# Startup loads of a window-attention and Fourier kernel: the table of positions moves to ScalarE's DMA queue, three weights move to SyncE's, and VectorE scales the odd heads' keys in three more rows

## The chip, the cores and the metric

The kernel runs on one core of one Trainium2 chip, as one program. The metric is the device time of one execution in microseconds (us). Before the change four runs took 3613.70, 3613.27, 3615.47 and 3615.18 us, a median of 3614.44.

A core has five engines that each follow their own stream of instructions in order: TensorE (PE) multiplies matrices and transposes, with its weight loads (PEld) beside the multiplications; VectorE (DVE) and ScalarE (ACT) do element-wise work; GpSimd (POOL) does element-wise work on data outside PSUM; SyncE (SP) does little but issue DMA transfers. In this kernel transfers are issued by SyncE and, at the start alone, by ScalarE; each of the two has a queue of its own (q1 and q10 in the profile). An engine that issues a transfer spends time of its own stream on it.

## The reference, cut to what matters

The input is 32 images of 56 x 56 positions with 128 channels, all in float32. Two layers follow one another, and each adds its result to its input:

```python
x = x + _L0_conv_ref(_gn(x), rpb_table, w_qkv, w_proj, b_proj)   # window attention
x = x + _L1_conv_ref(_gn(x), w0, w1, W1, b1, W2, b2)             # Fourier mixing, feed-forward
```

`_gn` is a group norm over 32 groups of 4 channels of one image. The first layer rolls the image by 3 in both directions, cuts it into 8 x 8 windows of 49 positions, and attends inside each window with 4 heads of 32 channels:

```python
attn = einsum('bhid,bhjd->bhij', q * scale, k) + bias[None] + mask
out  = einsum('bhij,bhjd->bihd', softmax(attn), v)
```

`bias` is gathered from the table of relative positions, `rpb_table` (169 x 4), one value for each pair of positions in a window and each head. `mask` is -100 between positions that the roll brought together. The second layer takes a cosine transform along each of the two axes, keeps 32 modes, multiplies each by a 128 x 128 matrix, transforms back, and applies a feed-forward net with 512 hidden channels.

## The kernel before, in words

**Tiling and stages.** An image has 8 rows of 8 windows, and a cycle of the main loop (line 1020) takes one row further. Image 0 goes through the attention alone, in `first_rows` (line 967, cycles 0 to 10). From cycle 11 on each cycle works on a row of attention of one image and on parts of the Fourier layer and feed-forward of the images before it, in `halves_first`, `eighths`, `quarters`, `full` and `halves_last`. Ahead of cycle 0 `image_groups` transposes image 0 in four groups of two rows (TensorE, line 276), ScalarE copies the result out (lines 288 to 294), VectorE gathers statistics (line 298), and `image_norm` (line 316) turns these into a factor for each channel, which ScalarE multiplies into the weights of queries, keys and values (`wn`, line 364).

**One row of attention.** `attn_qk` (line 372) multiplies the row by the weights of the queries and of the keys (helper at line 112) and copies both out of PSUM. The queries go out in one ScalarE pass (line 380). The keys go out twice, once with the odd heads set to zero and once with the even heads set to zero, by a factor of 0 or 1 per channel (`heads`) and a bias (`im.bias`): `k_sb[:, 0]` on ScalarE (line 389), and `k_sb[:, 1]` on ScalarE (line 393) where `first` is true, on VectorE (line 397) where it isn't. `first_rows` passes True and `halves_first` False. `attn_scores` (line 418) multiplies queries and keys, and VectorE adds the table `bm` to the result (line 439). Then follow the maximum (VectorE, line 449), its subtraction (POOL, line 450), the exponential (ScalarE, line 456), the sum and its reciprocal (VectorE, lines 461 and 463), and the multiplication (POOL, line 464). One cycle later the result is transposed (line 475), then multiplied by the values (line 500) and projected.

**The table `bm`.** `bm` holds bias plus mask for each kind of row and window. It is made at the start, in four steps. Seven small DMAs read the shifted table of positions into seven partitions (`rpb_cols`, line 166): those with an even index are issued on SyncE's queue, the odd ones on ScalarE's. Seven more spread this over 49 partitions (`rpb`, line 170), and one copies those to a second set of 49 (line 173). All of these eight are on SyncE's queue, and so are the four reads of the mask (line 181). VectorE then makes sixteen additions of bias and mask (line 191): eight on the first set of partitions and eight on the second. A second part of `bm`, for the last row of windows, is added by POOL in cycles 4 and 5.

**Other loads.** `load_image(0)` (line 126) issues five DMAs on SyncE's queue: half of image 0 (784 KB), most of the other half (672 KB), and three small pieces around the roll's edge. `const_load` (line 132) loads the constants: those named in `FIRST`, that is `gavg` (64 KB), `wqkv` (192 KB) and `bproj` (56 KB), on ScalarE's queue, all others on SyncE's. On SyncE's queue the tables of the cosine transforms, image 1 and the weights of the second layer follow.

**What sets the order.** The main loop stands inside `manual_schedule` for TensorE, ScalarE, VectorE and POOL: these keep the order in which it is written. What comes before the loop (the constants, `bm`) and everything on SyncE is placed by the framework's planner, which works with its own costs when the program is built. So SyncE's order, and the place of the sixteen additions in VectorE's stream, aren't written in the code. Waits between engines are made by the framework. The semaphores of the DMAs are handed out in turn, eight of them, over both queues together.

Of the kernel before, what the change touches and what calls it, by code (L numbers as in the profile page):

```python
# [48 lines left out]
def swin_fourier_kernel(  # L49
# [20 lines left out]
    nc = tc.nc  # L70
# [12 lines left out]
    def attn_bank():  # L83
        return bank("pa", 4)
# [23 lines left out]
    def halved(dst, lhsT, rhs, start=True, stop=True):  # L108

        for p in range(0, dst.shape[0], P // 2):  # L110
            ps = slice(p, min(p + P // 2, dst.shape[0]))
            nc.tensor.matmul(dst[ps], lhsT=lhsT[:, ps], rhs=rhs, start=start, stop=stop)  # L112
# [14 lines left out]

    FIRST = ("gavg", "wqkv", "bproj")  # L130

    def const_load(shape, src, name):
        t = const.tile(shape, F32, tag=name, name=name)
        (nc.scalar if name in FIRST else nc.sync).dma_start(t, src)
        return t

    ident = const.tile([P, P], F32, tag="ident", name="ident")
# [7 lines left out]
    gavg = const_load([P, P], group_avg, "gavg")  # L145
    wqkv = const_load([P, 3 * C], w_qkv_t, "wqkv")
    wproj = const_load([P, C], w_proj_t, "wproj")
    bproj = const_load([TC, C], b_proj.partition_broadcast(TC), "bproj")

# [7 lines left out]
    with nc.allow_non_contiguous_dma(reason="relative position bias, once"):  # L157


        cols = work.tile([P, 4, C], F32, tag="zT", name="rpb_cols").rearrange("p n c -> p (n c)")  # L160
        cols = cols[:WS, : NH * span * WS].rearrange("p (h y x) -> p h y x", h=NH, y=span)
        for ix in range(WS):
            src = bass.AP(
                rpb_rev.tensor, rpb_rev.offset + WS - 1 - ix, [[span, NH * span], [1, WS]]
            )
            (nc.scalar if ix % 2 else nc.sync).dma_start(
                cols[ix : ix + 1].rearrange("p h y x -> p (h y) x"), src.unsqueeze(0)
            )
        for iy in range(WS):
            nc.sync.dma_start(  # L170
                rpb[iy * WS : (iy + 1) * WS], cols[:, :, WS - 1 - iy : span - iy]
            )
# [37 lines left out]
    with nc.allow_non_contiguous_dma(reason="constant, once"):  # L210
        for blk in range(8):
# [4 lines left out]
            src = idct_h.rearrange("p (h r) -> p h r", r=4)[modes, :, 2 * li : 2 * li + 2]  # L216
# [85 lines left out]
    def image_bias(im, i):  # L302

        n0, n1 = WS * i // 2, WS * (i + 2) // 2
        for a, e in ((n0, n0 + 4), (n0 + 4, n1)):
            piece = im.x[:, a:e]
            nc.gpsimd.tensor_tensor(  # L307
                piece, piece, bproj.unsqueeze(1).to_broadcast([TC, e - a, C]), ALU.add
            )
# [62 lines left out]
    def attn_qk(im, i, first):  # L372

        n = RT if i else RT + 1
        q, src = q_sb, im.xw[i][:, :n]
        pq = attn_bank()
        halved(pq[:, :n], im.w[:, 0:C], src)
        if i == 0:
            nc.scalar.mul(im.bias[:, 0:1], pq[:, RT:n], QS)
        nc.scalar.activation(  # L380
            q[:, :RT], pq[:, :RT], AF.Identity, bias=im.bias[:, 0:1], scale=QS
        )
        pk = attn_bank()
        halved(pk[:, :n], im.w[:, C : 2 * C], src)
        if i == 0:
            for u in range(2):
                nc.scalar.mul(im.bias[:, 3 + u : 4 + u], pk[:, RT:n], heads[:, u : u + 1])
        pk3 = pk[:, :RT].rearrange("p (w j) -> p w j", j=WT)
        nc.scalar.activation(
            k_sb[:, 0], pk3, AF.Identity, bias=im.bias[:, 3:4], scale=heads[:, 0:1]  # L390
        )
        if first:
            nc.scalar.activation(
                k_sb[:, 1], pk3, AF.Identity, bias=im.bias[:, 4:5], scale=heads[:, 1:2]
            )
        else:
            nc.vector.tensor_scalar(
                k_sb[:, 1], pk3, heads[:, 1:2], im.bias[:, 4:5], ALU.mult, ALU.add
            )
# [18 lines left out]
    def attn_scores(im, i, r):  # L418

        q, a = q_sb, a_sb[r % 3]  # L420

        ps = [attn_bank(), attn_bank()]
        for pr in range(NP):
            for hp in range(2):
                cs = HALVES[hp]
                for e in range(2):
                    w = 2 * pr + e  # L430
                    nc.tensor.matmul(  # L431
                        ps[hp][HALVES[e], pr * 2 * WT : (pr + 1) * 2 * WT],
                        lhsT=q[cs, w * WT : w * WT + JP],
                        rhs=k_sb[cs, :, w],
                        start=True,
                        stop=True,
                    )
        for hp in range(2):
            nc.vector.tensor_tensor(  # L439
                a[:, 2 * hp : 2 * hp + 2, :, 0:WT].rearrange("p u w j -> p w u j"),  # L440
                ps[hp][:, :RT].rearrange("p (w u j) -> p w u j", u=2, j=WT),
                bm[:, i // (NWR - 1), hp],
                ALU.add,
            )

    def attn_max(r):
        a3 = a_sb[r % 3].rearrange("p t w j -> p (t w) j")[:, :, 0:WT]
        mx = small.tile([P, 2 * NWR], F32, tag="mx", name="mx")
        nc.vector.tensor_reduce(mx, a3, axis=AX.X, op=ALU.max)  # L449
        nc.gpsimd.tensor_tensor(  # L450
            a3, a3, mx.unsqueeze(2).to_broadcast([P, 2 * NWR, WT]), ALU.subtract
        )

    def attn_exp(r):
        a3 = a_sb[r % 3].rearrange("p t w j -> p (t w) j")[:, :, 0:WT]
        nc.scalar.activation(a3, a3, AF.Exp)  # L456

    def attn_divide(r):
        a3 = a_sb[r % 3].rearrange("p t w j -> p (t w) j")[:, :, 0:WT]
        sm = small.tile([P, 2 * NWR], F32, tag="sm", name="sm")  # L460
        nc.vector.tensor_reduce(sm, a3, axis=AX.X, op=ALU.add)  # L461
        rs = small.tile([P, 2 * NWR], F32, tag="rs", name="rs")
        nc.vector.reciprocal(rs, sm)  # L463
        nc.gpsimd.tensor_tensor(  # L464
            a3, a3, rs.unsqueeze(2).to_broadcast([P, 2 * NWR, WT]), ALU.mult
        )

    def attn_transpose(im, i, r):

        a = a_sb[r % 3]  # L470
        im.aT[i] = []
        for hf in range(2):
            pt = attn_bank()
            for h in range(NH):
                nc.tensor.transpose(  # L475
                    pt[:PW, h * P : h * P + PW],
                    a[:PW, h, 2 * hf : 2 * hf + 2].rearrange("p w j -> p (w j)")[:, :PW],
                    ident[:PW, :PW],
                )
            aT = work.tile([P, 4, P], F32, tag="aT", name="aT", bufs=4)  # L480
            src = pt[:PW].rearrange("p (m x) -> p m x", x=P)[:, :, :PW]
            if hf:
                nc.scalar.copy(aT[:PW, :, :PW], src)  # L483
            else:
                nc.vector.tensor_copy(aT[:PW, :, :PW], src)
            im.aT[i].append(aT)
# [335 lines left out]
    def row(r):  # L822
        return (images[r // NWR], r % NWR) if 0 <= r < NB * NWR else (None, 0)
# [143 lines left out]
    def first_rows(cycle, norm):  # L967
        im, i = row(cycle)
        if im:
            attn_qk(im, i, True)  # L970
        if cycle:
            attn_exp(cycle - 1)
        im3, i3 = row(cycle - 3)
        if im3:
            attn_values(im3, i3, cycle - 3)
        im2, i2 = row(cycle - 2)
        if im2:
            attn_transpose(im2, i2, cycle - 2)
        if cycle:
            attn_divide(cycle - 1)  # L980
        if im:
            attn_scores(im, i, cycle)
            attn_max(cycle)
        if im3:
            attn_project(im3, i3)
        next(norm, None)
        last, j = row(cycle - 4)
        if last:
            for _ in attn_sums(last, j):
                pass  # L990
        if im:
            attn_v(im, i, cycle)

        if cycle < NWR // 2:
            image_bias(im, 2 * cycle)
        elif cycle >= NWR - 2 and cycle < NWR + 2:
            image_bias(images[1], 2 * (cycle - NWR + 2))
        if cycle in (4, 5):
            for half in range(2):
                bias_and_mask(nc.gpsimd, 1, cycle - 4, half)  # L1000
        next_begin(cycle)
        next_groups(cycle)
        if cycle == CONV_BEGIN - 1:
            start_stats(im3)
            for _ in attn_sums(im3, i3):
                pass
            attn_exp(cycle)
            attn_divide(cycle)
            last, j = row(cycle - 1)
            attn_transpose(last, j, cycle - 1)  # L1010

    ET = mybir.EngineType
    with tc.manual_schedule(engines={ET.PE, ET.Activation, ET.DVE, ET.Pool}):
# [6 lines left out]
        for cycle in range(NB * NWR + CONV_BEGIN + FF_AT[-1] - NWR + 1):  # L1020
# [22 lines left out]
            b, i = divmod(cycle, NWR)  # L1043
# [65 lines left out]
```

## Time and profile before

| | |
|---|---|
| median of four runs | 3614.44 us |
| the profiled execution | 3613.70 us |
| its span, first to last instruction | 3611.8 us |
| TensorE busy | 3551.5 us (98%) |
| VectorE busy | 2251.4 us (62%) |
| ScalarE busy | 2144.3 us (59%) |
| POOL busy | 1374.1 us (38%) |
| DMA, mean rate over the span | 108 GB/s |

The profile is one execution, seen by the hardware's profiler. Times count from the first instruction. A busy share is a mean over the whole span. The chain of work is followed back from the last instruction: at each step to what released it, or to the instruction before it on the same engine. In a timeline row the first number is the start, the second the length. "x7" means seven instructions put together, and what stands in brackets is the engine's idle time before them with what ended it. SPq and ACTq are issues of DMAs by SyncE and ScalarE. In a list of waits the numbers are the sum, the count and the longest.

The first instructions of the start, as the timeline tells them: the image's DMAs are issued from 0.74 us on. TensorE begins its transposes at 7.09 us, when the first half has landed, and goes on with the second half at 10.62. VectorE's norm runs from 14.60 to 17.16, ScalarE writes the scaled weights at 17.90, the keys and queries are multiplied from 18.57, and the first scores from 23.11. The bias is first added at 26.29. The rows of image 0 then follow one another: the first maximum of image 0 (line 449) begins at 27.37, that of image 1 at 84.5. From image 3 on an image takes 110.1 to 112.8 us.

### The profile page before, as it was taken

The numbers are of one execution on the slowest core, as the hardware profiler recorded it, in microseconds if no ns is written. First come the engines' busy times: TensorE is split into PE (matmuls) and PEld (weight loads), VectorE is DVE, ScalarE is ACT, GpSimd is POOL, SyncE is SP. The second block draws the span as 40 slices with busy tenths as digits, with TensorE's granted clock in tenths as the row PEclk, the third lists the DMA queues.
The fourth block names the chain that finished last, engine by engine and source line by source line (L and its number), as shares of the span: only waits on it lengthen the run. The fifth ranks groups of instructions, "written<-read, shape, count | busy, mean of one in ns | idle before, by whom it ended". The sixth has DMA issues, their size and how long they took to land.

```text
span 3611.8 us, 161664 instructions
## 1 busy us (share of the span) xinstructions
PE 3551.5 (98%) x72192; PEld 2829.2 (78%) x72192; DVE 2251.4 (62%) x4722; ACT 2144.3 (59%) x4044; POOL 1374.1 (38%) x1437
## 2 busy tenths in 40 slices
PE   7899999999999999999999999999999999999999
PEld 5777778787878787887777787878877877777776
DVE  7766666666666666666656666666666666666641
ACT  5566565655666655666656665556665566655553
POOL 5443343433444333434334434343443344342421
PEclk9999999999999999999999999999999999999999
DMA  4334443444434444334444344443444443444343
GB/s 118 95 103 111 112 112 94 114 112 111 112 97 110 110 112 115 102 104 109 112 108 113 98 110 112 111 117 93 112 109 115 106 115 94 113 109 114 94 116 98
DMA packets 687349, 390.30 MB, mean 108 GB/s; under 512 B 39967, under 2 KB 657600, under 8 KB 686400
## 3 DMA queue, kind: packets, MB, share of 16 engines
q1 hardware_dynamic: 686045, 379.65, 38.9%
q8 instruction: 568, 9.31, 1.1%
q14 instruction: 125, 1.02, 0.1%
q10 hardware_dynamic: 611, 0.32, 0.0%
HBM read 218.29 MB, written 161.48 MB: 105 GB/s over the span
## 4 chain that ended last, share of the span: by engine, by line
PE 93%; DVE 4%; issue 1%; ACT 1%; POOL 1%; DMA 0%; SPq 0%; POOLq 0%; DVEq 0%; ACTq 0%
PE pc L112 38%; PE pa L112 15%; PE pa L409 6%; PE pc L680 6%; PE pa L475 6%; PE pc L646 6%; PE pa L431 5%; PE pa L500 4%; PE pc L719 4%; PE pa L276 1%; PE pc L276 1%; DVE a L439 1%; DVE xf L730 0%; DVE oT L531 0%; POOL rstd L617 0%
## 5 line engine op out<-in xcount | busy, mean ns | idle before, releaser
L450 POOL TENSOR_TENSOR a<-a,mx 128x784 f32<-128x784 f32 x256 | 389.3, 1521 | 1392.4 <-DVE mx L449 959.8
L112 PE MATMUL pc<-wff,hid 128*64 128x128 f32 x12544 | 740.3, 273 | 1.3 <-ACT hid L764 1.0
L112 PE MATMUL pc<-xf,wff 128*64 128x512 f32 (+2 forms) x3584 | 718.5, 540 | 1.1 <-DVE xf L730 1.0
L112 PEld LDWEIGHTS pc<-wff,hid 128*64 128x64 f32 x12544 | 702.7, 137 | 7.7 <-ACT hid L764 4.6
L461 DVE TENSOR_REDUCE sm<-a 128x16 f32<-128x784 f32 x256 | 248.2, 970 | 675.9 <-ACT a L456 672.4
L464 POOL TENSOR_TENSOR a<-a,rs 128x784 f32<-128x784 f32 x256 | 389.2, 1520 | 606.6 <-DVE rs L463 555.0
L764 ACT ACTIVATE hid<-pc,b1sb 128x512 f32<-128x512 f32 (+2 forms) x896 | 522.3, 631 | 72.4 <-PE pc L112 68.9
L112 PEld LDWEIGHTS pc<-xf,wff 128*64 128x64 f32 x3584 | 278.0, 137 | 356.6 <-issue 236.8
L380 ACT ACTIVATE q<-pa,bqkv 128x392 f32<-128x392 f32 x256 | 150.3, 587 | 463.8 <-PE pa L112 458.0
L112 PE MATMUL pa<-xw,wn 128*64 128x392 f32 (+1 forms) x2048 | 389.2, 495 | 9.3 <-ACT wn L364 8.3
L531 DVE TENSOR_SCALAR oT<-pa,bqkv 128x98 f32<-128x98 f32 (+2 forms) x768 | 171.3, 278 | 242.7 <-PE pa L500 242.6
L456 ACT ACTIVATE a<-a 128x784 f32<-128x784 f32 x256 | 222.7, 870 | 146.8 <-POOL a L450 144.8
L752 POOL TENSOR_TENSOR res<-res,b2sb 128x512 f32<-128x512 f32 (+2 forms) x256 | 264.2, 1037 | 113.8 <-DMA res<-scr 113.8
L416 ACT COPY v<-pa 128x512 f32<-128x512 f32 x256 | 151.0, 590 | 244.9 <-PE pa L409 244.8
L409 PE MATMUL pa<-wn,xw 128*64 128x128 f32 x4096 | 283.0, 280 | 5.4 <-issue 3.7
L307 POOL TENSOR_TENSOR xl<-xl,bproj 112x512 f32<-112x512 f32 (+1 forms) x256 | 287.1, 1144 | 0.0
L500 PEld LDWEIGHTS pa<-aT,v 49*32 49x32 f32 x16384 | 172.3, 105 | 145.2 <-issue 119.1
L439 DVE TENSOR_TENSOR a<-pa,bm 128x392 f32<-128x392 f32 x512 | 265.1, 561 | 25.9 <-PE pa L431 2.2
L483 ACT COPY aT<-pa 113x452 f32<-113x452 f32 x256 | 139.6, 545 | 209.8 <-PE pa L475 206.3
L409 PEld LDWEIGHTS pa<-wn,xw 128*64 128x64 f32 x4096 | 220.8, 137 | 38.0 <-issue 4.8
L449 DVE TENSOR_REDUCE mx<-a 128x16 f32<-128x784 f32 x256 | 246.6, 963 | 4.3
L788 DVE TENSOR_TENSOR res<-pc,res 128x512 f32<-128x512 f32 (+3 forms) x257 | 138.6, 550 | 174.9 <-PE pc L112 129.8
(97 smaller groups left out, 5748.8 us busy)
## 6 DMA issues: line engine op xcount, KB each, us to landing
zscr<-z SPq DMA_DIRECT2D x512, 112.0 KB
htok<-scr SPq DMA_DIRECT2D x256, 196.0 KB
zT<-zscr SPq DMA_DIRECT2D x192, 256.0 KB
res<-scr SPq DMA_DIRECT2D x160, 256.0 KB
out_dram<-res SPq DMA_DIRECT2D x160, 256.0 KB
scr<-xl SPq DMA_DIRECT2D x128, 224.0 KB
xl<-in_x_dram SPq DMA_DIRECT2D x32, 784.0 KB
xl<-in_x_dram SPq DMA_DIRECT2D x32, 672.0 KB
```

Of the source, the lines that this page charges most:

```text
L112: nc.tensor.matmul(dst[ps], lhsT=lhsT[:, ps], rhs=rhs, start=start, stop=stop)
L307: nc.gpsimd.tensor_tensor(piece, piece, bproj.unsqueeze(1).to_broadcast([TC, e - a, C]), ALU.add)
L409: nc.tensor.matmul(pv[hs, j * C : (j + 1) * C], lhsT=im.xw[i][:, w * WT : w * WT + JP], rhs=im.w[:, 2 * C : 3 * C], start=True, stop=True,)
L439: nc.vector.tensor_tensor(a[:, 2 * hp : 2 * hp + 2, :, 0:WT].rearrange("p u w j -> p w u j"), ps[hp][:, :RT].rearrange("p (w u j) -> p w u ...
L449: nc.vector.tensor_reduce(mx, a3, axis=AX.X, op=ALU.max)
L450: nc.gpsimd.tensor_tensor(a3, a3, mx.unsqueeze(2).to_broadcast([P, 2 * NWR, WT]), ALU.subtract)
L456: nc.scalar.activation(a3, a3, AF.Exp)
L461: nc.vector.tensor_reduce(sm, a3, axis=AX.X, op=ALU.add)
L464: nc.gpsimd.tensor_tensor(a3, a3, rs.unsqueeze(2).to_broadcast([P, 2 * NWR, WT]), ALU.mult)
L500: nc.tensor.matmul(po4[u][h * HD : (h + 1) * HD, 2 * f + e], lhsT=v[ks, 2 * f + e, h * HD : (h + 1) * HD], rhs=im.aT[i][f][ks, h, e * JP : ...
L752: nc.gpsimd.tensor_tensor(res[:m, c0:c1], res[:m, c0:c1], b2sb[:m].unsqueeze(1).to_broadcast([m, c1 - c0, C]), ALU.add,)
L764: nc.scalar.activation(hf[:, :n], ph[:, :n], AF.Relu, bias=b1sb[:, f : f + 1])
```

## The change

Three edits. `const_load` issues all its DMAs on SyncE's queue: `gavg`, `wqkv` and `bproj` now stand there behind the five DMAs of image 0, which come first in the code. All seven reads of the table of positions into `rpb_cols` are issued on ScalarE's queue, so they are the only DMAs that ScalarE issues. And `first_rows` passes `cycle > 2` for `first`: in cycles 0, 1 and 2 the keys of the odd heads are copied by VectorE (line 397) instead of ScalarE (line 393).

```diff
-    FIRST = ("gavg", "wqkv", "bproj")
-
     def const_load(shape, src, name):
         t = const.tile(shape, F32, tag=name, name=name)
-        (nc.scalar if name in FIRST else nc.sync).dma_start(t, src)
+        nc.sync.dma_start(t, src)
         return t
...
-            (nc.scalar if ix % 2 else nc.sync).dma_start(
+            nc.scalar.dma_start(
                 cols[ix : ix + 1].rearrange("p h y x -> p (h y) x"), src.unsqueeze(0)
             )
...
         if im:
-            attn_qk(im, i, True)
+            attn_qk(im, i, cycle > 2)
         if cycle:
             attn_exp(cycle - 1)
```

The line numbers in the text are those of the kernel before.

## The prediction

> **What bounds the kernel now.** I read the page's chain of work first, then the same chain over the first 30 us, where the edit lies, and then the records of the queues there.
>
> The page gives the chain that ended last over the whole span: TensorE carries it, and no DMA queue has a share worth a percent.
>
> ```profile
> PE 93%; DVE 4%; issue 1%; ACT 1%; POOL 1%; DMA 0%; SPq 0%; POOLq 0%; DVEq 0%; ACTq 0%
> ```
>
> Over the first 30 us the chain is another one (start, length, what):
>
> ```profile
> 1.19 9.38 DMA xl<-in_x_dram
> ...
> 14.95 0.88 SPq L170
> ...
> 22.36 2.40 DMA rpb<-rpb
> ...
> 24.79 0.84 DVE bm L191 x5
> ...
> 26.29 0.03 DVE a L439
> ```
>
> The first scores are added to the bias at 26.29, and what comes last there is the table of positions: seven gathers on SyncE's queue, one copy of the table, VectorE's sixteen additions. After 26.29 the rows of image 0 hang on one another and TensorE takes over. No view shows a later stage that waits for a load set in motion at the start, so what row 0 wins or loses goes through to the end at full size.
>
> The timeline of ScalarE, SyncE and TensorE over the same stretch shows the second path to 26.29 and who issues what:
>
> ```profile
> 2.36 2.89 ACTq L166 DMA_DIRECT2D rpb_cols<-in_rpb_rev_dram  x3
> 5.29 1.28 ACT L294 ACT_TABLE_LOAD   x1 [5.29 <-issue]
> 9.67 3.46 SPq L166 DMA_DIRECT2D rpb_cols<-in_rpb_rev_dram  x4
> 13.25 1.52 SPq L181 DMA_DIRECT2D mask<-in_shift_mask_dram  x4
> 14.95 5.76 SPq L170 DMA_DIRECT2D rpb<-rpb_cols  x7
> 22.38 0.68 ACT L393 ACTIVATE k<-pa,bqkv,heads 128x392 f32<-128x392 f32 x1
> 23.11 1.59 PE L431 MATMUL pa<-k,q 64*64 64x98 f32 x32 [1.65 <-ACT k L393]
> ```
>
> The scores of row 0 end at 24.70, so they stood ready 1.55 us before the bias did. That slack is the first number.
>
> **Image and weights (removed from ScalarE's queue).** The DMA view (packets, MB, share of the 16 engines) up to 7 us, and then up to 10.6 us, when the image's second half had landed (10.57):
>
> ```profile
> q1 hardware_dynamic: 1913, 0.97, 52.9%
> q10 hardware_dynamic: 291, 0.26, 19.2%
> ```
>
> ```profile
> q1 hardware_dynamic: 3346, 1.67, 65.6%
> q10 hardware_dynamic: 611, 0.32, 16.5%
> ```
>
> q1 is SyncE's queue, q10 is ScalarE's queue: gavg, wqkv and bproj, 0.32 MB, moved while the image was still on its way, at 245 GB/s (2 to 7 us) with the engines' share at 1.00. Behind the image on SyncE's queue they no longer do: 0.32 MB / 245 GB/s = 1.3 us, second half at 9.3. Bounds: 0 (if the tail at 8.1 to 10.6, only 196 GB/s, is a few slow engines) and 1.6 us (at that 196). I take 1.3, since the share stood at 0.95 or over to the end. The first half lands about 1 us sooner too, but that is worth little: ident_x is done at 6.27 and TensorE began at 7.09.
>
> The Trainium skill ("Trainium Kernel Development and Optimization", Key Constraints) says that DMAs of several issuing engines run on the same 16 DMA engines, so that spreading them saves only the sequencer's time. Read strictly it speaks against this step: the half would stay at 10.57, row 0 would begin its bias at 24.9, and the time would be 3613.0. It says nothing on order, and the q10 rows show weights moved ahead of the image.
>
> **Seven reads of the table on ScalarE's queue.** ScalarE issues DMAs ahead of its own work. Out go 0.42 + 0.66 + 0.45, and four reads come: 0.73 + 1.34 + 6 x 0.76 + gaps = 6.8, where it was 5.25 (line 166 on ScalarE took 1.34 us the first time, 0.76 the median). The table load (1.28) then ends at 8.1, exactly when the first copy began (8.11). Its four groups of copies take 1.0 us each, so two end at 10.1 and the third waits for the image: TensorE from 9.3, copy from 10.4 (11.66 before). So the image's 1.3 us survive; norm, wn (17.90), keys and scores come 1.3 earlier. The cover is thin: each further us on ScalarE's queue up to 1.3 eats into the gain one for one. What could add it is this line of SyncE's waits:
>
> ```profile
> SPq L118 <- DMA gavg<-in_group_avg_dram: 2.9, 1, 2.9
> ```
>
> The semaphores go round in eight, and an issue waits until the transfer eight issues before it has landed. The seventh read has a first or second issue as its forerunner (landed by 6), about when it would be issued anyway.
>
> **The table's path on SyncE.** Four reads leave (3.46), gavg, wqkv and bproj come (1.53 with gaps 1.65). The weights are not needed soon: wqkv at 17.90, bproj by POOL at 29.95, wproj at 43.87, gavg at 104. One of the four weights has the image's second half as its forerunner, so the last of them is issued about 10.4, and the reads, out by 6.8, have landed by then. Gathers: seven at 0.82, 10.5 to 16.3 (14.95 to 20.71 before). If the masks follow (1.52), the copy is issued at 17.9 and lands 2.40 later, 20.3 (24.76 before). If they go ahead as now, the gathers end at 17.9 and the small dct loads stand before the copy as now: 21.8. Then 1.48 for eight additions. I take 20.3, since the reads leave nothing to wait for that the masks would fill. What stands behind on SyncE (the dct and idct tables, image 1 from 37.3, read first at 53.5) moves up with it and has nobody waiting; if the queue were late instead, image 1's cover is the 6 us between its landing (47.05 for its second half) and that first read.
>
> **Odd heads' keys on VectorE, rows 0 to 2.** ScalarE's second key pass follows the first after 0.57 and ends at 23.06. VectorE's is taken from the later rows, view of line 397:
>
> ```profile
> L397 DVE TENSOR_SCALAR k<-pa,heads,bqkv x245: 672/684/689, 103.5 to 3456.4; 128x392 f32<-128x392 f32 x123
> ...
>   ACT k L389: 94.5, 122
> ```
>
> 122 times VectorE sat idle until ScalarE's first pass was over. In no record does L397 start less than 0.03 us after L389's end (205.89 + 0.68, then 206.60). The two do not run side by side: 0.03 + 0.68 against 0.57, so row 0 is 0.14 later, not sooner. In rows 1 and 2 the scores come 0.14 later as well, but the bias addition at 32.11 and 37.86 waits for the divisor (rs, L463), 1.35 and 1.7 us after the scores. VectorE's own 0.68 lies in its idle 2.53 and 1.46 before L461. ScalarE's freed 0.67 is worth nothing there: the exponential (30.03, 35.78) waits for POOL. The price is what it puts in VectorE's queue: if the second eight additions (L191) stand ahead of L397, row 0's scores wait for the table.
>
> **The sum.** Norm path: scores end at 24.70 - 1.3 + 0.14 = 23.5, bias from 23.6. Table path, L397 behind all additions: 20.3 + 1.48 + 0.71 + 1.59 + gaps = 24.2. L397 ahead: 23.6. With the copy landing at 21.8: 25.65 or 23.6. Gains against 26.29: 2.1, 2.7, 0.6, 2.7. I take 2.1, the likeliest planner's order. The profiled run took 3613.7 for a span of 3611.8, and the median is 3614.4, 0.7 above it; 3614.4 - 2.1 = 3612.3.
>
> **Rivals.**
> - *Little gained* (0.14): ScalarE's queue is held until 9.3 by a forerunner (copies from 11.1, norm 1.1 later than now, bias at 26.0), or the masks go ahead of the gathers and L397 stands behind all additions (25.65). Gain 0 to 0.6: 3613.8 to 3614.4.
> - *Slower* (0.14): VectorE's order puts the first additions ahead of the norm's statistics, as the planner sees the table sooner. L191 would wait for gathers and masks (18.7), and bn_aggr start at 20.25 instead of 14.60: 5.65 on the norm path less the slack of 1.55, so +4.1, 3618.5; with all sixteen ahead +5.6 to +7.1, or over if the copy is later still. It decides as soon as bn_aggr starts after 16.1. Against it: L191 stands behind nb (17.90) now, and SyncE has only one issue fewer ahead of the gathers.
> - *More* (0.08): full 2.7, and a stretch at half clock goes too. At 43.3 to 46.7 the granted clock was 0.50; L112, L409 and L431 of that row took 1.4 more than in the row at 59. 3610.3.
> - *The loop's order moves* (0.14): SyncE's order is planned, not written. If one issue changes places in each image, 0.24 us by 30 images is already 7.2, to either side. Against it: in the timeline of SyncE the 63 issues of an image are the same sequence for every image from 2 on, so it has settled in spite of an uneven start.
>
> Of the clock "TensorE: Matmul & The Clock Gate" (Part 1) says that its window runs freely, so that the same kernel meets it in another phase each time. The trace shows four half-clock stretches of 3.4 to 3.7 us, no phases.
>
> **How the numbers follow.** Forecast 0.50, the rivals as given. 0.2%, 7.2 us, is about what a measurement of this kernel can tell from no change. Forecast, little and more lie within it, and most of slower: 0.50 + 0.14 + 0.08 + 0.09 = 0.81. Slower by more: 0.05 + 0.07 = 0.12. Faster by more: 0.07. The range takes forecast, little and more (0.72) and the small values of the other two (some 0.08), which lie around no change: 3610.3 less the runs' scatter of 1.1 is 3609.2; 3614.4 plus one half-clock stretch (1.4) and 1.1 is 3616.9.
>
> **What would show it.** Right: the second half near 9.3, the table load ending near 8.1, gathers from about 10.5, the copy landing by 21.8, L439 at 23.6 to 24.9, L397 after L389. Wrong: L191 ahead of L334 on VectorE, ScalarE's copies after 9, or rows of image 2 and later that take another time than now.

## The result, and the profile after

The kernel after takes 3619.91 us (median of 31 runs, 3616.79 to 3625.28) where the kernel before takes 3613.47 (51 runs, 3609.45 to 3618.80; the four runs that the prediction started from had 3614.44). The ratio is 1.0019, with a 95% interval of 1.0014 to 1.0024. The change makes the kernel about 6.4 us slower. The prediction said 3612.3 with a range up to 3616.9: the time lies 3.0 us above the range, on the side of the rival called *Slower*. The profiled execution took 3617.67 us for a span of 3615.9.

Line numbers of the kernel after are lower by 2 than those of before from the constants' loads on (the additions are L189, the aggregate of the statistics L332, the odd heads' keys L395, the bias addition L437).

The page of after gives the same shares of the chain over the whole span as before, so nothing there tells of the loss:

```profile
PE 93%; DVE 4%; ACT 1%; issue 1%; POOL 1%; DMA 0%; SPq 0%; ACTq 0%; POOLq 0%; DVEq 0%
```

The chain over the first 40 us of after (start, length, what) does:

```profile
2.14 7.67 DMA rpb_cols<-in_rpb_rev_dram
...
18.23 1.94 DMA rpb<-rpb_cols
20.20 1.45 DVE bm L189 x8
21.65 0.29 DVE stat L332
...
23.32 1.48 DVE bm L189 x8
...
26.35 0.62 ACT wn L362
27.02 2.91 PE pa L112 x8
...
30.97 0.70 DVE k L395
31.71 1.59 PE pa L429 x32
```

Before, the table of positions and the norm were two paths that met at the bias addition. Now they are one path: the table comes first, then the additions (L189), and only behind them the norm, the scaled weights, the keys and the scores. VectorE's timeline of before and of after shows the exchange:

```profile
13.48 1.08 DVE L298 BATCH_NORM_STATS2 st<-xw 128x6 f32<-128x392 f32 x2 [0.22 <-ACT xw L294]
14.60 0.37 DVE L334 BATCH_NORM_AGGREGATE stat<-st 128x2 f32<-128x48 f32 x1
...
17.90 0.16 DVE L361 SCALAR_TENSOR_TENSOR nb<-back,rstd 128x1 f32<-128x1 f32 x1 [0.75 <-POOL rstd L356]
22.04 1.45 DVE L191 TENSOR_TENSOR bm<-rpb,mask 49x98 f32<-49x98 f32 x8 [3.98 <-DMA rpb<-rpb_cols]
24.79 1.48 DVE L191 TENSOR_TENSOR bm<-rpb,mask 49x98 f32<-49x98 f32 x8 [1.30 <-DMA rpb<-rpb]
26.29 1.04 DVE L439 TENSOR_TENSOR a<-pa,bm 128x392 f32<-128x392 f32 x2
```

```profile
12.22 3.84 DVE L296 BATCH_NORM_STATS2 st<-xw 128x6 f32<-128x392 f32 x8 [5.94 <-ACT xw L292]
20.20 1.45 DVE L189 TENSOR_TENSOR bm<-rpb,mask 49x98 f32<-49x98 f32 x8 [4.14 <-DMA rpb<-rpb_cols]
21.57 0.36 DVE L332 BATCH_NORM_AGGREGATE stat<-st 128x2 f32<-128x48 f32 x1
...
23.32 1.47 DVE L189 TENSOR_TENSOR bm<-rpb,mask 49x98 f32<-49x98 f32 x8
...
26.35 0.16 DVE L359 SCALAR_TENSOR_TENSOR nb<-back,rstd 128x1 f32<-128x1 f32 x1 [0.75 <-POOL rstd L354]
30.97 0.69 DVE L395 TENSOR_SCALAR k<-pa,heads,bqkv 128x392 f32<-128x392 f32 x1 [4.46 <-ACT k L387]
33.33 1.04 DVE L437 TENSOR_TENSOR a<-pa,bm 128x392 f32<-128x392 f32 x2 [1.68 <-PE pa L429]
```

The first eight additions, which stood behind the norm, now stand ahead of the aggregate (L332), and the second eight stand in the middle of the norm. Both wait in VectorE's stream, which is in order, and so does all that follows. The bias addition moves from 26.29 to 33.33, 7.04 later. Worked out along the path: the aggregate starts 6.97 later (14.60 to 21.57); from it to `wn` takes 4.78 instead of 3.30, since the second eight lie between (+1.48); from `wn` to the scores takes 5.36 instead of 5.21 (+0.15, the keys); and from the scores to the bias 1.62 instead of 3.18, since the table is there by now (-1.56). The sum is 7.04. The medians differ by 6.4, the two profiled executions by 4.0. Part of the difference can be seen in the rows behind the start: the maximum of row 3 begins 7.23 later than in before, that of row 4 only 5.68 later, since a stretch of before in which TensorE's granted clock was 0.50 (43.28 to 46.69) isn't found there in after. What follows shifts by some us from one profile to the next.

The second thing that the prediction had otherwise is ScalarE. Its timeline after, and the issues of SyncE, in one answer:

```profile
0.73 9.64 ACTq L164 DMA_DIRECT2D rpb_cols<-in_rpb_rev_dram  x7
0.74 9.41 SPq L118 DMA_DIRECT2D xl<-in_x_dram  x5
...
10.40 1.28 ACT L292 ACT_TABLE_LOAD   x1 [10.40 <-DMA rpb_cols<-in_rpb_rev_dram]
...
11.70 0.48 ACT L292 COPY xw<-pa 128x392 f32<-128x392 f32 x1
...
13.06 5.94 SPq L168 DMA_DIRECT2D rpb<-rpb_cols  x7
```

ScalarE is out of its seven reads only at 10.37, and the first copy of the transposed image begins at 11.70 instead of 8.11. Its sixth read is issued at 6.66 and its seventh at 9.62: each waited for a semaphore that a half of the image holds (an issue waits until the transfer eight issues earlier, its forerunner, has landed). SyncE is held in turn by the reads: the waits of its queue in after name them twice.

```profile
SPq L118 <- DMA rpb_cols<-in_rpb_rev_dram: 4.9, 2, 2.6
```

So the statistics end at 16.06 instead of 14.56. By then VectorE waits for the table anyway, until 20.20.

### The profile page after: what moved, and what is told of

Read it like the earlier page. It is cut to its first block, busy times and chain, and to the rows that moved or that the text cites. A ratio compares the mean times of both kernels' runs of the same rounds, so it can differ in the third digit from the quotient of the medians.

```text
span 3615.9 us, 161658 instructions
## 1 busy us (share of the span) xinstructions
PE 3549.4 (98%) x72192; PEld 2825.1 (78%) x72192; DVE 2251.0 (62%) x4725; ACT 2143.8 (59%) x4041; POOL 1374.0 (38%) x1437
## 4 chain that ended last, share of the span: by engine, by line
PE 93%; DVE 4%; ACT 1%; issue 1%; POOL 1%; DMA 0%; SPq 0%; ACTq 0%; POOLq 0%; DVEq 0%
PE pc L112 38%; PE pa L112 15%; PE pa L407 6%; PE pc L678 6%; PE pa L473 6%; PE pc L644 6%; PE pa L429 5%; PE pa L498 4%; PE pc L717 4%; PE pa L274 1%; PE pc L274 1%; DVE a L437 1%; DVE xf L728 0%; DVE oT L529 0%; POOL rstd L615 0%
## 5 line engine op out<-in xcount | busy, mean ns | idle before, releaser
L437 DVE TENSOR_TENSOR a<-pa,bm 128x392 f32<-128x392 f32 x512 | 265.1, 560 | 26.8 <-PE pa L429 3.1
```

What stands on the lines that cost most here:

```text
L437: nc.vector.tensor_tensor(a[:, 2 * hp : 2 * hp + 2, :, 0:WT].rearrange("p u w j -> p w u j"), ps[hp][:, :RT].rearrange("p (w u j) -> p w u ...
```

## The experiments

Theory: the loss is the place of the additions in VectorE's order. Rivals: ScalarE is held by its reads, and that delays all; or the keys on VectorE cost it; or the table itself is late. The runs of one group share a chip and the runs of before there, whose medians are 3609.92 (first group, e1 to e4), 3608.38 (e5 to e8) and 3608.75 (e9 and e10), so only ratios within a group are compared. The start of row 0's bias addition (26.29 in before) is read from one profile each and is the sharper number, but the rows behind it shift against before by several us from profile to profile, which the start doesn't explain.

**e1 and e2: the additions written behind the norm.** The additions leave the planner's hands and follow the three steps of the norm inside the scheduled part. e2 also gives the odd heads' keys back to ScalarE.

```diff
--- after.py
+++ e1_after_behind
-    for t in range(2):
-        for half in range(2):
-            bias_and_mask(nc.vector, 0, t, half)
...
         for _ in range(3):
             next(norm)
+        for half in range(2):
+            for t in range(2):
+                bias_and_mask(nc.vector, 0, t, half)
```

```diff
--- e1_after_behind
+++ e2_after_behind_actkeys
-            attn_qk(im, i, cycle > 2)
+            attn_qk(im, i, True)
```

> The changed kernel, with VectorE's sixteen additions of bias and mask written into its stream behind the norm of image 0 (where the kernel before had them) instead of left to the planner. Order theory (the additions ahead of and inside the norm hold it up): the norm's aggregate begins at 16.1 as soon as ScalarE's late copies allow (21.57 in the changed kernel), wn at 19.4, and row 0's bias is limited by the table and by the keys behind it: copy lands at 23.2, additions to 24.8, keys 25.5, scores 27.1, bias at about 27.2 (33.33 changed, 26.29 before); total within 2 us of the kernel before. Hold theory (ScalarE kept by its reads until 10.4 is the cause): bias stays at 30 or later, total stays 4 us or more above before.

> As the run before, and the odd heads' keys of rows 0 to 2 back on ScalarE. If the keys' only price is their place in VectorE's queue behind the additions and behind ScalarE's first pass: row 0's scores end at 26.2 and the bias follows at 26.3, 0.9 sooner than with the keys on VectorE. If the keys on VectorE were a gain: bias later than there, at 27.8.

e1 takes 3611.52 us, a ratio of 1.0004 (0.9996 to 1.0013); e2 takes 3608.34, 0.9997 (0.9988 to 1.0006). VectorE in e1:

```profile
15.68 0.37 DVE L329 BATCH_NORM_AGGREGATE stat<-st 128x2 f32<-128x48 f32 x1
...
19.75 1.45 DVE L189 TENSOR_TENSOR bm<-rpb,mask 49x98 f32<-49x98 f32 x8 [0.61 <-DMA rpb<-rpb_cols]
...
22.61 1.48 DVE L189 TENSOR_TENSOR bm<-rpb,mask 49x98 f32<-49x98 f32 x8 [1.40 <-DMA rpb<-rpb]
24.12 0.69 DVE L392 TENSOR_SCALAR k<-pa,heads,bqkv 128x392 f32<-128x392 f32 x1
25.80 1.04 DVE L434 TENSOR_TENSOR a<-pa,bm 128x392 f32<-128x392 f32 x2 [1.00 <-PE pa L426]
```

With the additions behind the norm the loss is gone, though ScalarE is held nearly as long as in after (its copies begin at 11.28, there at 11.70). The bias is added at 25.80, 7.5 sooner than in after, and 1.4 sooner than expected. ScalarE's hold is thus no cause of the loss by itself.

The two runs were to differ by the keys, but the bias comes 6.82 and 6.83 us after `wn` in them. This doesn't make the keys free. In e1 they end 0.68 later, counted from `wn`, and the scores' multiplications then take 0.90 us; in e2 they take 1.59. The granted clock was 1.00 there in e1, until 25.86, and 0.50 in e2 (the first line is e1's, the second e2's):

```profile
24.86 0.90 PE L426 MATMUL pa<-k,q 64*64 64x98 f32 x32 [2.32 <-DVE k L392]
24.50 1.59 PE L426 MATMUL pa<-k,q 64*64 64x98 f32 x32 [1.65 <-ACT k L388]
```

The phase of the clock hid the price, and these two can't give it; e4 and e9 do.

**e3: the kernel before, with only VectorE's order of after.** No load is moved.

```diff
--- before.py
+++ e3_before_ahead
-    for t in range(2):
-        for half in range(2):
-            bias_and_mask(nc.vector, 0, t, half)
...
+        if im.b == 0:
+            for t in range(2):
+                bias_and_mask(nc.vector, 0, t, 0)
         nc.vector.bn_aggr(stat[:, 0:2], im.st)
...
         average(mean[:, 1], turned)
+        if im.b == 0:
+            for t in range(2):
+                bias_and_mask(nc.vector, 0, t, 1)
```

> The kernel before, with only the order of VectorE's stream changed to that of the changed kernel: eight additions ahead of the norm's aggregate, eight ahead of its second average's end. Queues and keys as before. Order theory: the aggregate waits for the gathers (first additions at 22.04), begins at 23.5 instead of 14.60; the norm is 8.9 late plus 1.5 for the second eight, scores end at 35.1, bias at 35.1: 8.8 us later than before and the total 7 to 9 us up. Hold theory: the total stays within 2 us of before, since ScalarE is not held here.

It takes 3616.70 us, a ratio of 1.0021 (1.0012 to 1.0030), against 1.0019 of the whole change. VectorE:

```profile
21.62 1.45 DVE L191 TENSOR_TENSOR bm<-rpb,mask 49x98 f32<-49x98 f32 x8 [7.51 <-DMA dct_h<-in_dct_dram]
23.00 0.35 DVE L334 BATCH_NORM_AGGREGATE stat<-st 128x2 f32<-128x48 f32 x1
24.95 1.48 DVE L191 TENSOR_TENSOR bm<-rpb,mask 49x98 f32<-49x98 f32 x8
33.92 0.57 DVE L442 TENSOR_TENSOR a<-pa,bm 128x392 f32<-128x392 f32 x1 [5.98 <-PE pa L434]
```

VectorE idles 7.51 us in front of the statistics' aggregate, which would have had all that it needs at about 14. The order alone gives +7.63 at the bias. That is less than the 8.8 expected, since the aggregate began 0.5 sooner than expected and the scores took 0.90 instead of 1.59. (The row names a transfer of the cosine table as what ended the wait. The additions don't read it: releasers are inferred from semaphores, and the transfers share eight of these in turn.) With e1 this shows the cause from both sides: the order without the loads loses it all, the loads without the order lose nothing that can be measured.

**e4, e5, e6: each edit alone, on the kernel before.**

```diff
--- before.py
+++ e4_keys
-            attn_qk(im, i, True)
+            attn_qk(im, i, cycle > 2)
--- before.py
+++ e5_weights
-        (nc.scalar if name in FIRST else nc.sync).dma_start(t, src)
+        nc.sync.dma_start(t, src)
--- before.py
+++ e6_table
-            (nc.scalar if ix % 2 else nc.sync).dma_start(
+            nc.scalar.dma_start(
```

> The kernel before with the third edit alone: odd heads' keys by VectorE in rows 0 to 2. My theory: VectorE's key pass stands behind the sixteen additions (last ends at 26.26), so it runs 26.3 to 27.0, scores 27.0 to 28.6, bias at 28.6: 2.3 later than before. Rival (the prediction's price): 0.14 later at the scores and nothing at the bias, which waits for the table anyway: bias at 26.3.

> The kernel before with the first edit alone: gavg, wqkv and bproj behind the image on SyncE's queue; reads still split, keys on ScalarE. ScalarE issues three reads, no read has a forerunner among the image's transfers, and the planner leaves the sixteen additions behind the norm. Expected: second half of the image at about 9.6 (10.57 before), aggregate at 13.6 (14.60), wn at 16.9; SyncE issues three weights more ahead of its four reads, so gathers 15.5 to 21.2, copy landing at 25.1, bias at 26.6 (26.29 before): the image's 1 us is won and lost again on the table; total within 2 us of before. If the weights' place on the queue were what costs: bias at 30 or later.

> The kernel before with the second edit alone: all seven reads on ScalarE's queue, behind gavg, wqkv and bproj. The seventh read's forerunner is a small piece of the image. Hold theory: ScalarE is held until about 12, its copies start at 13.4 (8.11 before), the statistics end at 17.8. Order theory: the planner now puts eight additions ahead of the norm's last step (ve), which waits for the gathers until 21.9. Together wn at 22.8, bias at 29.6, 3.3 later than before, total 2 to 5 us up. If reads on ScalarE's queue are free: copies at 8.1 and bias sooner than 26.3.

e4 takes 3615.40 us, 1.0014 (1.0005 to 1.0023). In VectorE's stream L397 stands behind all sixteen additions:

```profile
25.41 1.48 DVE L191 TENSOR_TENSOR bm<-rpb,mask 49x98 f32<-49x98 f32 x8 [1.47 <-DMA rpb<-rpb]
26.92 0.69 DVE L397 TENSOR_SCALAR k<-pa,heads,bqkv 128x392 f32<-128x392 f32 x1
29.28 1.04 DVE L439 TENSOR_TENSOR a<-pa,bm 128x392 f32<-128x392 f32 x2 [1.67 <-PE pa L431]
```

The bias comes at 29.28, +2.98: the additions began 0.62 later in this profile, and the other 2.36 are the keys (0.69 and a gap) and the scores (1.58), which used to run beside the table's path and now follow it. The granted clock was 0.50 during these scores, so at full clock the price would be some 0.7 lower.

e5 takes 3609.66, 1.0003 (0.9994 to 1.0012). TensorE begins the second half of the image at 9.67 (10.62 before), and the aggregate starts at 13.12 (14.60). But SyncE now issues the weights ahead of the gathers, which begin at 15.81 (14.95), and the bias comes at 27.05, +0.75 (26.6 was expected). The norm's gain lies in front of a wait for the table. In this kernel the planner leaves the additions behind the norm.

e6 takes 3612.28, 1.0010 (1.0001 to 1.0019). Here ScalarE issues three weights and seven reads, and waits for transfers of SyncE's queue in between:

```profile
2.37 10.53 ACTq L166 DMA_DIRECT2D rpb_cols<-in_rpb_rev_dram  x7
12.92 1.28 ACT L294 ACT_TABLE_LOAD   x1 [12.92 <-DMA mask<-in_shift_mask_dram]
14.21 0.48 ACT L294 COPY xw<-pa 128x392 f32<-128x392 f32 x1
```

The first eight additions stand ahead of the norm's `ve` (L352) at 22.40, and the bias comes at 31.50, +5.20 and 1.9 later than expected, as ScalarE was held for longer. So one edit alone moves the additions not at all (e4, e5) or by less (e6); the order of after was seen only with all three edits. That the first two suffice is likely, but no run has them without the third in a kernel whose additions the planner places.

**e7: five reads on ScalarE's queue instead of seven, on top of e2.** This tells what holds ScalarE.

```diff
--- e2_after_behind_actkeys
+++ e7_five_behind_actkeys
-            nc.scalar.dma_start(
+            (nc.scalar if ix < 5 else nc.sync).dma_start(
```

> The second run of the first set (additions behind the norm, keys on ScalarE), with five reads on ScalarE's queue and two on SyncE's. No read then has a transfer of the image as its forerunner. Hold theory: ScalarE's table load starts at about 5.2 instead of 10.3, copies at 7.8 instead of 11.6, aggregate at 13.6 instead of 16.0, wn at 16.9 instead of 19.3. The bias gains nothing by it, as SyncE's two reads put the table at 26.6. If something else keeps ScalarE (TensorE, the image): copies stay at 11 or later.

```profile
0.73 4.50 ACTq L164 DMA_DIRECT2D rpb_cols<-in_rpb_rev_dram  x5
5.27 1.28 ACT L289 ACT_TABLE_LOAD   x1 [5.27 <-issue]
7.50 0.48 ACT L289 COPY xw<-pa 128x392 f32<-128x392 f32 x1 [0.95 <-PE pa L271]
```

The hold is gone: the copies begin at 7.50 instead of 11.59, and the aggregate at 12.71 instead of 15.99. The time is 3608.67 us, 1.0000 (0.9991 to 1.0008), and the bias comes at 25.81, 0.31 sooner than in e2 only: 3.3 us won on the norm's path end in front of the table, whose first additions come at 21.75 instead of 19.99.

**e9: the kernel after with five reads instead of seven, and nothing else.** The same line as in e7, changed in after. The planner then puts all sixteen additions behind the norm by itself.

> The kernel after, with one number changed: five of the seven reads of the table on ScalarE's queue, two on SyncE's. The planner then puts all sixteen additions behind the norm, and no read on ScalarE's queue has a forerunner among the image's transfers. Theory (the loss is ScalarE held, and the additions ahead of the statistics): table load about 5.3, first copy 7.5, bn_aggr 12.7, wn 16.0. What is left is the price of the keys in VectorE's queue: additions end about 25.8, keys to 26.5, scores to 28.1, bias 28.2; ratio to the kernel before about 1.0005, some 4.5 us less than the kernel after. Rival (the table itself comes late when its reads stand on ScalarE's queue, whatever the order): bias at 33, ratio 1.0019 as after.

```profile
12.88 0.37 DVE L332 BATCH_NORM_AGGREGATE stat<-st 128x2 f32<-128x48 f32 x1
...
24.34 1.48 DVE L189 TENSOR_TENSOR bm<-rpb,mask 49x98 f32<-49x98 f32 x8 [1.48 <-DMA rpb<-rpb]
25.85 0.69 DVE L395 TENSOR_SCALAR k<-pa,heads,bqkv 128x392 f32<-128x392 f32 x1
...
28.20 1.04 DVE L437 TENSOR_TENSOR a<-pa,bm 128x392 f32<-128x392 f32 x2 [1.67 <-PE pa L429]
```

The bias comes at 28.20, as expected (28.2), and the time is 3612.59 us, 1.0010 (1.0000 to 1.0019), where 1.0005 was expected. Against e7 the bias is 2.39 later, and the keys are what differs behind the norm: the same price as e4's 2.36, again with the scores at a granted clock of 0.50.

Whether the keys cost more than this in rows 1 and 2 stays open. e4 takes 5.5 us more than before for a bias 2.98 later, and e9 3.8 for 1.91; e1 takes 3.2 more than e2, whose bias comes 0.32 later than e1's. But each median is known to about 3 us against before, so these differences don't show a second price.

**e8 and e10: a shorter start.** The second is the first once more. Five reads on ScalarE's queue; on SyncE's the image, two reads, `wqkv`, the gathers, and the other weights behind them; the additions behind the norm as in e1; the keys on ScalarE.

```diff
--- before.py
+++ e8_shorter_start
-        (nc.scalar if name in FIRST else nc.sync).dma_start(t, src)
+        nc.sync.dma_start(t, src)
...
-            (nc.scalar if ix % 2 else nc.sync).dma_start(
+            (nc.scalar if ix < 5 else nc.sync).dma_start(
                 cols[ix : ix + 1].rearrange("p h y x -> p (h y) x"), src.unsqueeze(0)
             )
+        wqkv = const_load([P, 3 * C], w_qkv_t, "wqkv")
...
+    bproj = const_load([TC, C], b_proj.partition_broadcast(TC), "bproj")
+    wproj = const_load([P, C], w_proj_t, "wproj")
+    gavg = const_load([P, P], group_avg, "gavg")
...
```

> An attempt to keep the gain on both paths: five reads on ScalarE's queue, two on SyncE's right behind the image, then wqkv alone, then masks and gathers; bproj, wproj and gavg behind these; additions behind the norm; keys on ScalarE. Norm path as in the run before (scores end at 23.7); gathers 13.4 to 19.2, copy landing at 23.3, additions to 24.8, bias at 24.9: 1.4 sooner than before. Total 1 to 3 us below the kernel before, which the runs can hardly tell from it. Rival: the table's path is as long as ever and the bias comes at 26 or later.

> The shortened start once more, unchanged, to narrow its interval. Its bias at 25.1 again (26.3 before), which is worth 1.2 us: a ratio of 0.9997, and an interval of about 0.999 to 1.0005. If the 2.6 us of the first time were the start's, 0.9993 again.

The bias comes at 25.06 and 24.80. The times are 3605.75 us, 0.9993 (0.9984 to 1.0002), and 3605.70, 0.9992 (0.9983 to 1.0001). Both are faster than after. Against before each interval just takes in no change; that two groups give 2.6 and 3.1 us makes a gain likely, but it is more than the 1.2 and 1.5 us that the start shows, and where the rest would come from stays open.

## Why the prediction was wrong

**The step that failed** is the order that the sum was made for. It took "the likeliest planner's order", with the additions behind the norm, and set against the rival *Slower* that L191 stood behind nb, "and SyncE has only one issue fewer ahead of the gathers". The planner put the first eight ahead of the aggregate and the second eight inside the norm, and the aggregate began at 21.57 instead of 14.60. The argument counted issues on SyncE, which doesn't settle the place of an instruction without a written order: e5's weights leave the additions where they were, e6's reads put half of them ahead of the norm's last steps, the kernel after with all three edits has all sixteen inside or ahead of the norm, and five reads instead of seven (e9) put them back. By what rule the planner does this, the runs don't show. No view of the profile before shows what the planner will do; what could be read from it was what each order costs.

**The rival *Slower*** had the mechanism, and gave the point from which it decides (an aggregate after 16.1; it was 21.57). Its price was +4.1 for the first eight and +5.6 to +7.1 for all sixteen; measured +7.04. At a chance of 0.14 it was left out of the range at the upper end, and that is why the range missed. With the order open, both orders belonged in it.

**Image and weights: right in kind, a little too large.** TensorE began the second half at 9.65 instead of 10.62, 0.97 sooner where 1.3 was taken. Over all profiles it began at 10.16 to 10.98 with the weights on ScalarE's queue (before, e3, e4, e6) and at 8.99 to 9.72 with them behind the image (after and the other seven), so the gain is sure, and its size only to about half a us. The Trainium skill ("Trainium Kernel Development and Optimization", Key Constraints) says that such transfers interleave, and that spreading them over queues saves only the time to issue them; the prediction's strict reading of this left the half at 10.57. The runs disagree with that reading: e5, which moves the weights alone, has 9.67.

**Seven reads on ScalarE's queue: wrong.** "The seventh read has a first or second issue as its forerunner (landed by 6)": the sixth had the image's first half, the seventh its second, so ScalarE was out at 10.37 and not at 6.8. It was named under *Little gained* with copies from 11.1; measured 11.70. In after this cost nothing further, as the aggregate waited for the table until 21.57.

**The table's path on SyncE: too early by 2.6.** The gathers were to begin at 10.5 and began at 13.06. SyncE itself waited 4.9 us for reads of ScalarE's queue, so the weights went out from 10.19 to 12.16, and two masks followed. The copy was issued at 20.76, and the second eight additions, which read it, start at 23.32; the forecast had it landed at 20.3, or 21.8 at most.

**Keys: right.** L395 starts 0.03 after L387's end, and costs 0.15 where 0.14 was forecast, because in after the additions are done by then. That L397 behind the additions puts the scores behind the table was in the sum too (24.2 against 23.6), and e4 and e9 show it: 2.36 and 2.39 us.

**The loop's order** didn't move: from 200 us on SyncE issues the same sequence of transfers in both profiles. **The clock:** the half-clock stretch at 43.3, which the rival *More* expected to go, was indeed gone in the profile of after, and row 4 is 1.55 nearer to before than row 3; with the start 7.04 late that couldn't show as a gain. The clock records of before begin only at 26.21, so the four stretches of the prediction leave out the start. The 32 multiplications of the scores took 1.59 us at 23.11 in before and 0.91 at 29.86, so the clock was probably low at the start there too, and the 1.59 in the sum is probably the price at half clock.

**From the start to the end.** That row 0's loss "goes through to the end at full size" held roughly: 7.04 at the bias, 6.4 in the medians, and 7.63 and 6.8 in e3.

## What to carry to other kernels

Where part of the work is placed by a planner and part in a written order, a moved load can change the place of an instruction on another engine that runs in order, as it did here; price every place that it can take, give all of them room in the range, and where the place matters, write it (here one moved loop removed the whole loss). Where semaphores are handed out in turn over all queues, as in this kernel, a transfer moved to a compute engine's queue can make that engine wait for other queues' transfers; count the forerunners by what they carry, not by when they were issued.

## What the runs showed of the hardware that was not expected

**A 1.4 KB read takes as long as the image beside it.** The second read was issued at 2.14 and landed 7.67 us later, at 9.81 (the first line of the chain of after). In the trace its semaphore is raised first at 3.31, and then not until 8.96 to 9.81, about when the semaphore of the image's second part is raised (8.50 to 9.60). The first read's is raised at 2.19 and then with that of the first half (5.94 to 6.91; the half's own 5.64 to 6.63). The data waited too. The DMA view of after, up to 7.9 us (first two lines) and for ScalarE's queue up to 9.0 us (the third):

```profile
q1 hardware_dynamic: 2755, 1.40, 78.9%
q10 hardware_dynamic: 65, 0.00, 0.5%
q10 hardware_dynamic: 390, 0.01, 2.6%
```

The seven reads make 455 packets, 65 each. Those of one read moved by 5.6 us, none from there to 7.9, and those of five between 7.9 and 9.0, when SyncE's queue had little of the image left. The Trainium skill ("DMA: Bandwidth & Descriptors", Queues, rings and completion order) says that a DMA engine takes the queues in turns, a packet of each. By short turns the small reads would pass early, which this gap doesn't show; why they waited, no run here tells.

**The clock stays low while TensorE waits.** In the profile of after, the granted clock by stretches, TensorE's busy time and number of matmuls ahead of it:

```profile
12.00:16.00 4.00, 0.00 (x0) 0.83 0.34 92
16.00:20.00 4.00, 0.00 (x0) 0.50 0.04 7
20.00:24.00 4.00, 0.00 (x0) 0.50 0.16 35
24.00:28.00 4.00, 0.98 (x4) 0.50 0.39 9
```

It is at 0.50 for 20.5 us, from 14.64 to 35.12, past row 0's scores. These took 1.59 us there, but the same in before (23.11), and 0.90 in e1. Against before the stretch costs little here: rows 1 and 2 begin their maxima 7.29 later than in before, row 0 7.04. But e1 and e2 show that 0.7 us of such a phase can hide or feign a term of that size.
